# Attention and depthwise convolution in one kernel: longer groups, statistics ahead, and normalisation moved between engines

## The chip, the cores and the metric

One core of one Trainium2 chip runs the kernel. The metric is the device time of one execution in microseconds (us); the time of the kernel before is the median of 3 runs. The core has five engines that run their own instruction streams in order: TensorE (PE; its weight loads are shown apart as PEld), VectorE (DVE), ScalarE (ACT), GpSimd (POOL) and SyncE (SP). SP, ACT and POOL also issue DMAs; the queue of an engine is meant when "SP's queue" is said.

## The reference

Input x is (16, 384, 32, 32) in float32. Two layers follow each other, each on a group-normalised input (32 groups of 12 channels, per image) and with a residual:

```python
x = x + attention(gn(x), w_qkv, w_proj, b_proj)   # 8 heads of 48, 1024 tokens per image
x = x + dwconv7x7(gn(x), w_sym)                   # w_sym = mean of the weight's four rotations
```

The attention is softmax(q k^T / sqrt(48)) v, then a projection with a bias. The second group norm needs the whole image after the first layer.

## The kernel before, in words

Everything is float32. An image is three tiles of 128 channels x 1024 pixels (index k or o, NK = 3). Heads go in pairs: image b has four units u = 4b + p, and a unit has 16 steps n (two halves h of the queries, eight blocks i of keys). A step is one score product (s_step, L325: two matmuls into a PSUM tile of two banks, then ScalarE's exponential, L339) and one value product (av_step, L341, into an accumulator of its half). V carries a column of ones, so the sums of the exponentials come out as one row of the accumulator. `take` (L355) copies a finished half out of PSUM. The softmax's maximum isn't subtracted; a check at the end (L816) would start a second, general program (L613) if a sum were out of range, and in the runs here it isn't taken.

PSUM is three tiles ("s", L130) that scores, q/k, v and projection products rotate through, and two accumulators. The score product of step k therefore waits for the exponential of step k - 3.

After a unit, its sums go to DRAM and back as columns (sums_out, L361), VectorE inverts them (L372), they go out and come back spread over rows (L377), and VectorE divides (L383). After four units, proj_step (L393) makes three projection products from three tiles of o, into which the fourth unit's rows have been packed by DMA (L388); ScalarE adds the bias (L406), and a DMA on GpSimd's queue adds the residual x in place (L407). That is x1.

The group norms (class Stats, L188): bn_stats on VectorE per channel (L195), a trip through DRAM that gathers the 12 channels of a group into a row (L201, L203), an aggregate on VectorE (L208), 1/sigma by four one-column instructions on GpSimd (ve_x, L210 to L214, with a power of -0.5), and a trip back that spreads scale and shift over channels (L216, L220). For image 0's x and image 15's x1 there is a short way, groups_on_pe (L224): averages by small matmuls against mask blocks. `apply` (L259) normalises a tile: x by ScalarE, x1 into a tile xn by GpSimd (L261).

The convolution is 49 taps (conv_tap, L452): VectorE multiplies a shifted window of xn by one weight per channel and adds it into x1. 44 of the 48 tiles go this way; the tiles k = 1, 2 of images 14 and 15 (PE_TILES) are done by TensorE (conv_on_pe, L544), from shifted copies that are stored (conv_store, L526) and loaded again (L534), all of it after the last attention step. out is stored by GpSimd's queue (conv_end, L464).

The order on every engine is the order of the program text, written by a planner at build time. It keeps two clocks, `clock` for TensorE and `vclock` for VectorE, with fixed costs per piece of work. `after(wait, cost, f)` (L664) puts VectorE work into a heap with a due time; `catch_up(to)` (L691) emits due work and else taps, until vclock reaches `to`. The main loop (L858) goes over groups of GS = 4 steps: four score products, then four value products, then either a projection (`project`, L727) or, as a credit allows, up to two chunks of the next image's q/k (qk_step, L273) or v (v_step, L301), then catch_up. Image b + 1's x is loaded (begin_x, L761) when image b's last v chunk is out, since x has one buffer; it is loaded on SP's queue (L150), its statistics and norm follow through the heap. v has two buffers. The first image's q, k, v are all issued ahead of its steps. The last image ends in a different way (L922 on): sums by a matmul with ones (divide_at_once, L415), projection in four parts from unpacked o (proj_part, L425, with the weights w_proj_4), residual and bias on VectorE (L439), groups_on_pe.

Of the kernel before, what the change touches and what calls it, by code (L numbers as in the profile page):

```python
# [10 lines left out]
F32 = mybir.dt.float32  # L11
# [33 lines left out]
def kernel(  # L45
# [64 lines left out]
    def run(general):  # L110
        tag = "g" if general else "f"
        with ExitStack() as stack:
# [11 lines left out]
            epool = pool("epool", 6)  # L124
# [13 lines left out]
            PE_K = [NK - 1, NK - 2]  # L138
            PE_TILES = [(b, k) for b in (B - 2, B - 1) for k in PE_K]

# [6 lines left out]
            def load_x(b):  # L147
                xns[b] = xpool.tile([P, NK, N], F32, tag="x", name=f"x_{b}")
                for k in range(NK):
                    nc.sync.dma_start(  # L150
                        xns[b][:, k, :], x[b, k * P : (k + 1) * P].rearrange("p h w -> p (h w)")
                    )
# [12 lines left out]
            nc.sync.dma_start(wp, w_proj_t.rearrange("(k p) c -> p k c", p=P))  # L165
# [7 lines left out]
            vs = []  # L173
            for i in range(2):
                t = wpool.tile([P, NT, VW], F32, name=f"v_{i}")
                nc.gpsimd.memset(t, 1.0)
                vs.append(t)
# [4 lines left out]
            mhalf = wpool.tile([P, NK], F32, name="mhalf")  # L182
            nc.gpsimd.memset(mhalf, -0.5)

# [3 lines left out]
            class Stats:  # L188
# [16 lines left out]
                def groups(self):  # L205
# [3 lines left out]
                    ve = small.tile([GROUPS, 1], F32, tag="ve", name=f"ve_{self.name}")  # L209
                    nc.gpsimd.tensor_scalar(ve, mv[:, 1:2], EPS, None, ALU.add)  # L210
                    af = small.tile([GROUPS, 2], F32, tag="af", name=f"af_{self.name}")
                    nc.gpsimd.tensor_tensor(af[:, 0:1], ve, mhalf[0:GROUPS, 0:1], ALU.pow)
                    nc.gpsimd.tensor_tensor(af[:, 1:2], mv[:, 0:1], af[:, 0:1], ALU.mult)
                    nc.gpsimd.tensor_scalar(af[:, 1:2], af[:, 1:2], -1.0, None, ALU.mult)  # L214
# [9 lines left out]
                def groups_on_pe(self, masks):  # L224
# [29 lines left out]
                    nc.gpsimd.tensor_tensor(self.sc[:, :, 0], d, mhalf, ALU.pow)  # L254
# [4 lines left out]
                def apply(self, dst, src, k, engine=None):  # L259
# [11 lines left out]
                    )  # L271

# [28 lines left out]
            def v_step(b, t2):  # L301
# [11 lines left out]
                for j in range(2):  # L313
                    dst = vs[b % 2][:, 2 * t2 + j, 0 : HEADS * (D + 1)]
                    nc.scalar.copy(  # L315
                        dst.rearrange("p (h d) -> p h d", d=D + 1)[:, :, 0:D],
                        ps[:, j, 0:C].rearrange("p (h d) -> p h d", d=D),
                    )

            def v_of(u, i, j):  # L320
                b, p = divmod(u, NP)
                c = (2 * p + j) * (D + 1)
                return vs[b % 2][:, i, c : c + 64]
# [90 lines left out]

            def divide_at_once(u, h):  # L415
# [6 lines left out]

            late, pps = {}, {}
# [28 lines left out]
            def conv_tap(b, k, dy, dx):  # L452
                (oy, iy), (ox, ix) = region(dy, dx)
                acc = x1s[b, k].rearrange("p (h w) -> p h w", w=W)[:, oy, ox]
# [199 lines left out]
            clock, vclock = 0.0, 0.0  # L654
# [3 lines left out]
            GS = 4  # L658
            PER_B = 2 * NT * NP

            def now():
                return max(clock, vclock)
# [7 lines left out]
            def us_tap(dy, dx):  # L670
                late_us = 0.06 if active[0][0] >= B - 2 else 0.0
                return ((H - abs(dy)) * (W - abs(dx)) + (130 if len(active) > 1 else 270)) / 940 + late_us

            def tap():
# [3 lines left out]
                if not active:  # L678
                    return 0.0
                b, k, n = active[0]  # L680
                took = us_tap(*TAPS[n])
# [8 lines left out]

            def catch_up(to):  # L691
                nonlocal vclock
                while vclock < to:
# [8 lines left out]
                    else:  # L702
                        vclock = min([to] + [t[0] for t in later[:1]])

# [21 lines left out]

            def project(b):  # L727
# [6 lines left out]
            def x1_part(b, k):  # L734
# [4 lines left out]
                if k == NK - 1:  # L739
                    st.gather()  # L740
                    after(7.0, 0.8, lambda: x1_groups(b, st))

            def x1_groups(b, st):
                st.groups()
                after(9.0, 0.0, lambda: x1_chains(b, st))

            def x1_chains(b, st):
                on_pe = [t for t in PE_TILES if t[0] == b]
                for k in range(NK - 1, -1, -1):
                    tail = b == B - 1  # L750
                    conv_begin(st, b, k, (nc.gpsimd, None, nc.vector)[k] if tail else nc.gpsimd)
# [9 lines left out]
            def begin_x(b):  # L761
                load_x(b)
                after(10.0, 3.8, lambda: x_channels(b))

            def x_channels(b):
# [4 lines left out]
                after(12.0, 0.8, lambda: x_groups(b, st))  # L770

            def x_groups(b, st):
                st.groups()
                after(35.0, 0.0, lambda: x_apply(b, st))

            def x_apply(b, st):
                for k in range(NK):
                    st.apply(xns[b][:, k, :], xns[b][:, k, :], k)
                ready[b] = now() + 6.0

            def finish(u):
                sums_out(u)
                if u < U - 1:
                    after(7.0, 0.3, lambda: finish2(u))
# [5 lines left out]
            def finish3(u):  # L790
                b, p = divmod(u, NP)
                divide(u)
                if p == NP - 1:
                    proj.append((now() + 4.0, b))

            def queue(b):
                chunks.extend(("qk", b, i) for i in range(4))
                chunks.extend(("v", b, i) for i in range(2))
                chunks.extend(("qk", b, i) for i in range(4, 6))
                chunks.extend(("v", b, i) for i in range(2, 4))  # L800
# [5 lines left out]
            st.groups_on_pe(masks_0.rearrange("p (b c) -> p b c", c=P))  # L806
# [5 lines left out]
            while chunks:  # L812
                issue(chunks.popleft())
            vclock = clock
# [41 lines left out]

            credit = 0.0
            for n0 in range(0, NS, GS):  # L858
                b, r = divmod(n0, PER_B)
# [5 lines left out]
                for n in range(n0, n0 + GS):  # L865
                    s_step(n)
                if n0 == NS - 2 * GS:
                    after(3.5, 4.2, lambda: None)
                    divide_at_once(U - 1, 0)
                if n0 == NS - GS:  # L870
                    for o in range(NK):
                        proj_part(B - 1, o, (0, 1))
# [123 lines left out]
```

## Time and profile before

| what | value |
|---|---|
| median of 3 runs | 3024.0 us (3023.43 to 3024.72) |
| the profiled execution | 3021.88 us, its span 3020.0 us |
| PE, DVE, ACT, POOL busy | 98%, 87%, 43%, 24% of the span |
| scores L331, values L347 on PE | 948.6 us, 935.4 us |
| q/k L280, v L306, projection L398 on PE | 506.8, 254.5, 235.7 us |
| taps L455 on DVE | 2379.2 us, 2156 of them |
| exponentials L339 on ACT | 967.0 us, 1024 of them |
| xn L261 on POOL | 198.0 us, 46 of them, 4309 ns mean |
| ve_x L210 on POOL | 313.8 us, 30 of them, 10461 ns mean |
| mean clock granted to PE | 0.994 |

The span runs from the first to the last instruction that the profile shows. In a group's line stand the source line, the engine, the operation, output and input tiles by their names in the program, the count, then the busy time in us and the mean of one in ns; a time in brackets is how long the engine was idle before it, and what ended that. An engine's busy time counts overlapping instructions once. In the stretches, PEclk is the share of full speed that TensorE's clock was granted.

### The profile page before, as it was taken

What the parts mean: (1) busy time and instruction counts of PE and PEld (TensorE: products, weight loads), DVE (VectorE), ACT (ScalarE), POOL (GpSimd) and SP (SyncE); (2) the same over time, 40 slices, a digit from 0 to 9 for tenths busy, and PEclk for the clock granted to TensorE, in tenths of its full rate; (3) what the DMA queues carried; (4) which work ended last, traced back from release to release, by engine and by line L of the source; (5) the groups of instructions that cost most, each with busy time, mean ns of one, the idle gap of its engine ahead of it and who ended that gap; (6) DMA issues with size and microseconds to landing.
All of it is one profiled execution on the core that took longest, in us unless ns stands there. A gap on an engine that the chain in (4) does not pass through costs nothing.

```text
span 3020.0 us, 30559 instructions
## 1 busy us (share of the span) xinstructions
PE 2970.3 (98%) x11658; PEld 1166.2 (39%) x11658; DVE 2616.1 (87%) x2553; ACT 1298.7 (43%) x1469; POOL 728.3 (24%) x426
## 2 busy tenths in 40 slices
PE   7999999999999999999999999999999999999978
PEld 4333343433334343343434334343433434333333
DVE  1101898997999999999999999999999999999788
ACT  1534535354453545435353453535445353544400
POOL 1021004020140604215060320505133060411500
PEclk9999999999999999999999999999999999999989
DMA  2113031121312112131211313122131312212234
GB/s 70 38 23 67 15 66 37 39 53 33 67 36 58 23 52 51 36 70 39 52 30 36 66 36 66 42 46 37 36 66 36 66 37 51 37 43 38 89 83 114
DMA packets 68332, 149.42 MB, mean 49 GB/s; under 512 B 30880, under 2 KB 33168, under 8 KB 66640
## 3 DMA queue, kind: packets, MB, share of 16 engines
q1 hardware_dynamic: 47536, 90.80, 12.2%
q0 software_dynamic: 18560, 52.31, 7.8%
q10 hardware_dynamic: 2080, 4.26, 0.6%
q8 instruction: 94, 1.54, 0.2%
q14 instruction: 62, 0.51, 0.1%
HBM read 99.35 MB, written 29.49 MB: 43 GB/s over the span
## 4 chain that ended last, share of the span: by engine, by line
PE 90%; DVE 5%; issue 3%; POOL 1%; DMA 1%; ACT 0%; POOLq 0%; SPq 0%; DVEq 0%
PE ps_s L331 29%; PE acc L347 29%; PE ps_qk L280 16%; PE ps_v L306 8%; PE ps_proj L398 8%; DVE x L455 4%; POOL ve_x L210 1%; DMA wc<-in_w_conv 0%; PE ps_st_x L236 0%; DVE bs_x L195 0%; DMA out<-x 0%; DVE x L570 0%; DMA sums<-sum 0%; DMA sum<-o 0%; DVE o L383 0%
## 5 line engine op out<-in xcount | busy, mean ns | idle before, releaser
L455 DVE SCALAR_TENSOR_TENSOR x<-xn,wsym,x 128x960 f32<-128x960 f32 (+9 forms) x2156 | 2379.2, 1175 | 19.5 <-POOL xn L261 17.6
L339 ACT ACTIVATE e<-ps_s 128x1024 f32<-128x1024 f32 x1024 | 967.0, 1030 | 395.0 <-PE ps_s L331 390.1
L331 PE MATMUL ps_s<-qk 48*128 48x512 f32 x4096 | 948.6, 602 | 2.2 <-ACT e L339 2.2
L347 PE MATMUL acc<-e,v 128*64 128x512 f32 x4096 | 935.4, 598 | 0.0
L331 PEld LDWEIGHTS ps_s<-qk 48*128 48x128 f32 x4096 | 373.1, 186 | 566.8 <-issue 430.6
L347 PEld LDWEIGHTS acc<-e,v 128*64 128x64 f32 x4096 | 271.5, 136 | 632.4 <-issue 561.0
L280 PE MATMUL ps_qk<-x,wqk 128*128 128x512 f32 x1152 | 506.8, 596 | 2.3 <-DVE x L261 2.3
L407 POOL DMA_DIRECT2D x<-in_x x45 | 39.6, 881 | 1414.8 <-ACT x L406 1414.8
L280 PEld LDWEIGHTS ps_qk<-x,wqk 128*128 128x128 f32 x1152 | 217.0, 190 | 284.9 <-issue 278.3
L210 POOL TENSOR_SCALAR ve_x<-mv_x 32x1 f32<-32x1 f32 x30 | 313.8, 10461 | 44.4 <-DVE mv_x L208 43.3
L287 ACT COPY qk<-ps_qk 128x1024 f32<-128x1024 f32 x96 | 97.2, 1012 | 463.4 <-PE ps_qk L280 463.4
L306 PE MATMUL ps_v<-wv,x 128*128 128x384 f32 x768 | 254.5, 488 | 0.0
L398 PE MATMUL ps_proj<-o,wp 128*128 128x512 f32 x540 | 235.7, 595 | 0.2 <-DVE bs_x L195 0.2
L358 ACT COPY o<-acc 128x512 f32<-128x512 f32 x128 | 75.1, 587 | 307.2 <-PE acc L347 307.2
L261 POOL TENSOR_SCALAR xn<-x,sc_x 128x1024 f32<-128x1024 f32 x46 | 198.0, 4309 | 33.5 <-DMA sc_x<-gr_x 33.1
L195 DVE BATCH_NORM_STATS2 bs_x<-x 128x6 f32<-128x512 f32 x192 | 120.2, 680 | 98.8 <-DMA x<-in_x 98.7
L306 PEld LDWEIGHTS ps_v<-wv,x 128*128 128x128 f32 x768 | 144.7, 190 | 113.6 <-issue 20.3
L372 DVE RECIPROCAL rec<-sums 128x16 f32<-128x16 f32 x63 | 15.8, 250 | 185.4 <-DMA sums<-sum 185.3
L398 PEld LDWEIGHTS ps_proj<-o,wp 128*128 128x128 f32 x540 | 101.4, 190 | 134.4 <-issue 131.4
L315 ACT COPY v<-ps_v 128x384 f32<-128x384 f32 x128 | 55.1, 483 | 196.9 <-PE ps_v L306 196.9
L406 ACT ACTIVATE x<-ps_proj,bp 128x1024 f32<-128x1024 f32 x45 | 50.1, 1114 | 192.6 <-PE ps_proj L398 175.0
L383 DVE TENSOR_TENSOR o<-o,inv 128x1024 f32<-128x1024 f32 x63 | 76.6, 1216 | 55.5 <-DMA inv<-inv 34.0
(70 smaller groups left out, 486.1 us busy)
## 6 DMA issues: line engine op xcount, KB each, us to landing
inv<-inv SPq DMA_DIRECT2D x126, 256.0 KB
x<-in_x SPq DMA_DIRECT2D x48, 512.0 KB
x<-in_x POOLq DMA_DIRECT2D x48, 512.0 KB, 5.5
out<-x POOLq DMA_DIRECT2D x48, 512.0 KB, 3.5
qk<-qk SPq DMA_DIRECT2D x96, 128.0 KB
sh<-xd SPq DMA_DIRECT2D x38, 160.0 KB
o<-o SPq DMA_DIRECT2D x90, 64.0 KB
sh<-xd ACTq DMA_DIRECT2D x26, 160.0 KB
```

The source lines that it names most:

```text
L195: nc.vector.bn_stats(self.bs[:, k, 6 * h : 6 * h + 6], src[:, h * HALF : (h + 1) * HALF])
L210: nc.gpsimd.tensor_scalar(ve, mv[:, 1:2], EPS, None, ALU.add)
L261: engine.tensor_scalar(dst, src, self.sc[:, k, 0:1], self.sc[:, k, 1:2], ALU.mult, ALU.add)
L280: nc.tensor.matmul(ps[:, h, :], lhsT=wqk[:, k, s, t, :], rhs=xns[b][:, k, h * HALF : (h + 1) * HALF], start=(k == 0), stop=(k == NK - 1),)
L287: nc.scalar.copy(halves(qks[u][:, s, :]), ps)
L306: nc.tensor.matmul(ps[:, j, 0:C], lhsT=xns[b][:, k, t * P : (t + 1) * P], rhs=wv[:, k, :], start=(k == 0), stop=(k == NK - 1),)
L331: nc.tensor.matmul(ps[:, j, :], lhsT=qks[u][r, 1, i * P : (i + 1) * P], rhs=qks[u][r, 0, h * HALF : (h + 1) * HALF], start=True, stop=True,)
L339: nc.scalar.activation(es[n], ps, AF.Exp, scale=SCALE)
L347: nc.tensor.matmul(accs[u, h][64 * j : 64 * j + 64, :], lhsT=v_of(u, i, j), rhs=e[:, j, :], start=(i == 0), stop=(i == NT - 1),)
L383: nc.vector.tensor_tensor(os_[u], os_[u], invs.pop(u), ALU.mult)
L398: nc.tensor.matmul(ps[:, h, :], lhsT=wp[:, t, o * P : (o + 1) * P], rhs=os_[NP * b + t][:, h * HALF : (h + 1) * HALF], start=(t == 0), sto ...
L455: nc.vector.scalar_tensor_tensor(acc, xn1s[b, k].rearrange("p (h w) -> p h w", w=W)[:, iy, ix], wsym[:, k, dy + PAD, dx + PAD : dx + PAD + 1],
```

## The change

- **Groups.** An image's 64 steps go in groups of 7, the last of 8, with eight exponential buffers instead of six. A projection or chunks may now follow the score half of a group as well as the value half (`other`).
- **v** has one buffer. The four v chunks of image b are issued together behind the first score half of image b, and only then is x of image b + 1 loaded.
- **x of images 1 to 15** is loaded on GpSimd's queue.
- **Statistics of x for images 2 to 15** are made during image 0: their tiles are loaded once more on GpSimd's queue into x1's buffers, bn_stats is taken, and all scales are computed in one go and kept (x_sc). Image 1 keeps its own way.
- **ScalarE normalises** x1 as well as x (image 0 and 15's x1 on three engines), at a fixed place: behind a group's score half, one image's norm at a time (`applies`).
- **1/sigma** in Stats.groups: a bit-trick first value and three Newton steps on VectorE, in place of the four GpSimd instructions.
- **Image 0 ends like image 15** (FAST): four-part projection, residual on VectorE, groups_on_pe behind the first score half of image 1. Its weights are loaded at the start and replaced in image 1.
- **The last image's end** is reordered: the fourth unit's second half is divided between parts of the projection. The lone tile (15, 0) is summed into two accumulators in turn (tap_of_two).
- Costs and waits of the planner change with it.

```diff
-            epool = pool("epool", 6)
+            epool = pool("epool", 8)
...
+            FAST = (0, B - 1)
+            LONE = (B - 1, 0)
...
+                queue = nc.gpsimd if b else nc.sync
                 for k in range(NK):
-                    nc.sync.dma_start(
+                    queue.dma_start(
...
+            def inverse_sigma(dst, mean, var, name):
+                nc.vector.tensor_scalar(half, var, EPS, 0.5, ALU.add, ALU.mult)
+                nc.vector.tensor_scalar(
+                    y.bitcast(I32), half.bitcast(I32), 1, None, ALU.logical_shift_right
+                )
+                nc.vector.tensor_scalar(
+                    y.bitcast(I32), y.bitcast(I32), -1.0, float(MAGIC), ALU.mult, ALU.add
+                )
+                for _ in range(3):
+                    nc.vector.tensor_tensor(t, y, y, ALU.mult)
+                    nc.vector.tensor_tensor(t, t, half, ALU.mult)
+                    nc.vector.scalar_tensor_tensor(y, t, 1.5, y, ALU.subtract, ALU.mult)
+                nc.vector.tensor_tensor(dst[..., 1], mean, y, ALU.mult)
+                nc.vector.tensor_scalar(dst[..., 0], y, -1.0, None, ALU.mult)
...
+            def stream_in(b, k):
+                many[b, k] = rpool.tile([P, N], F32, tag="x1", name=f"xs_{b}_{k}")
+                nc.gpsimd.dma_start(
+                    many[b, k], x[b, k * P : (k + 1) * P].rearrange("p h w -> p (h w)")
+                )
+            def stream_stats(b, k):
+                t = many.pop((b, k))
+                for h in range(2):
+                    nc.vector.bn_stats(
+                        many["bs"][:, b - 2, k, 6 * h : 6 * h + 6], t[:, h * HALF : (h + 1) * HALF]
+                    )
...
+            SIZES = [7] * 8 + [8]
...
             def x1_groups(b, st):
                 st.groups()
-                after(9.0, 0.0, lambda: x1_chains(b, st))
+                applies.append((now() + 10.0, lambda: x1_chains(b, st)))
...
-                    conv_begin(st, b, k, (nc.gpsimd, None, nc.vector)[k] if tail else nc.gpsimd)
+                    conv_begin(st, b, k, (nc.gpsimd, None, nc.vector)[k] if b in (0, B - 1) else None)
...
             def begin_x(b):
                 load_x(b)
-                after(10.0, 3.8, lambda: x_channels(b))
+                if b == 1:
+                    after(10.0, 3.8, lambda: x_channels(b))
+                else:
+                    applies.append((now() + 14.0, lambda: x_apply(b, None)))
...
+            for n, bk in enumerate(every):
+                after(4.0 * n, 0.0, lambda bk=bk: stream_in(*bk))
+                after(4.0 * n + 10.0, 1.3, lambda bk=bk: stream_stats(*bk))
+            after(4.0 * len(every) + 14.0, 0.0, stream_gather)
+            after(4.0 * len(every) + 34.0, 3.6, stream_groups)
...
+            def fast_finish(b):
+                proj_part(b, 0, (NP - 2,))
+                divide_at_once(NP * b + NP - 1, 1)
+                for o in range(1, NK):
+                    proj_part(b, o, (NP - 2,))
+                x1_stats[b] = Stats(f"x1_{b}")
+                for o in range(NK):
+                    proj_part(b, o, (NP - 1,))
+                    residual(b, o)
+                    x1_stats[b].channels(x1s[b, o], o)
...
+                for n in range(n0, n0 + size):
                     s_step(n)
+                if r == 0 and b - 1 == FAST[0]:
+                    fast_end(b - 1)
+                if r == 0:
+                    for i in range(NT // 2):
+                        issue(("v", b, i))
+                ending = b in FAST and r + size == PER_B
+                if ending:
+                    catch_up(clock)
+                    divide_at_once(NP * b + NP - 1, 0)
                     for o in range(NK):
-                        proj_part(B - 1, o, (0, 1))
+                        proj_part(b, o, (0, 1))
+                else:
+                    if applies and applies[0][0] <= clock:
+                        applies.popleft()[1]()
+                    other(r + size)
+                for n in range(n0, n0 + size):
                     av_step(n)
...
+                if ending:
+                    catch_up(clock)
+                    fast_finish(b)
+                else:
+                    other(r + size)
```

## The prediction

> **What bounds the kernel now.** First the page, busy time (its first part) and the chain that ended last (its fourth).
>
> ```profile
> PE 2970.3 (98%) x11658; PEld 1166.2 (39%) x11658; DVE 2616.1 (87%) x2553; ACT 1298.7 (43%) x1469; POOL 728.3 (24%) x426
> PE 90%; DVE 5%; issue 3%; POOL 1%; DMA 1%; ACT 0%; POOLq 0%; SPq 0%; DVEq 0%
> ```
>
> TensorE is the bound. Second, stretches of one image in the steady part (columns: stretch, then busy us and count of PE, weight loads, DVE, ACT, POOL, then clock, DMA share, GB/s).
>
> ```profile
> 963.70:1141.80 178.10, 178.10 (x670) 69.50 (x668) 174.68 (x169) 81.33 (x92) 53.09 (x25) 1.00 0.20 47
> ```
>
> An image costs 178.1 us of TensorE, and VectorE has 174.7 us of work in it: two engines 3.4 us apart. A saving on TensorE counts only if VectorE's work falls too.
>
> Third, the timeline of TensorE and of its weight loads, to see what a group of four costs beyond its matmuls (start, duration, idle before).
>
> ```profile
> 161.69 3.70 PE L331 MATMUL ps_s<-qk 48*128 48x512 f32 x16
> 165.32 3.65 PE L347 MATMUL acc<-e,v 128*64 128x512 f32 x16
> 168.90 3.70 PE L331 MATMUL ps_s<-qk 48*128 48x512 f32 x16
> ```
>
> ```profile
> 164.00 0.19 PEld L331 LDWEIGHTS ps_s<-qk 48*128 48x128 f32 x2 [0.29 <-ACT e L339]
> 165.32 0.20 PEld L347 LDWEIGHTS acc<-e,v 128*64 128x64 f32 x4 [0.76 <-issue]
> 168.90 0.30 PEld L331 LDWEIGHTS ps_s<-qk 48*128 48x128 f32 x4 [0.81 <-issue]
> ```
>
> A group lasts 168.90 - 161.69 = 7.21 us. Inside a half, weight loads come 0.429 us apart, eight intervals a half, so 16 x 0.429 = 6.86 us is matmul. The rest, 0.35 us, is lost at the two turns between scores (L331) and values (L347), where the weight load shows the 0.76 and 0.81 us gaps.
>
> Fourth, the timeline at the end: TensorE, GpSimd and VectorE.
>
> ```profile
> 2869.79 3.65 PE L347 MATMUL acc<-e,v 128*64 128x512 f32 x16
> 2875.34 1.10 PE L418 MATMUL ps_sum<-o,masks 128*128 128x512 f32 x2 [1.90 <-DVE inv L420]
> 2878.31 8.09 PE L431 MATMUL ps_proj<-o,wp 128*128 128x512 f32 x12 [1.87 <-DVE o L383]
> ...
> 2898.20 7.53 PE L431 MATMUL ps_proj<-o,mat 128*128 128x512 f32 x10 [10.94 <-DVE o L421]
> 2905.66 5.98 PE L557 MATMUL ps_conv<-sh,mat 128*32 128x512 f32 x56
> ```
>
> ```profile
> 2788.99 38.41 POOL L210 TENSOR_SCALAR ve_x<-mv_x 32x1 f32<-32x1 f32 x1 [12.72 <-DVE mv_x L208]
> ```
>
> ```profile
> 2846.16 1.22 DVE L383 TENSOR_TENSOR o<-o,inv 128x1024 f32<-128x1024 f32 x1 [18.85 <-ACT e L339]
> ```
>
> From the last value product (2873.4) to the first convolution piece (2905.66) TensorE takes 32.2 us for 17.5 us of matmuls. The cause lies 85 us earlier: a one-column GpSimd addition (ve_x) takes 38.4 us while VectorE runs taps; so xn of image 14 is late; SP waits to store it (a 29.9 us wait at L527) with the inverse sums queued behind it; VectorE stands idle 18.85 us; its taps slip, and the reciprocal that TensorE needs at 2878 comes at 2894. After that 100 us of convolution on TensorE set the end; VectorE stops with it.
>
> **Turns.** 16 groups an image become 9: 16 x 7 = 112 fewer turns x 0.35 = **-39.2 us**, all on the path. Does ScalarE follow a run of seven? In the same timeline exponentials start 1.24 us after the first score (1000.97, 1002.21) and 4 take 3.77 us: the first 1.03, later ones 0.913 each, against 0.858 for a score step. With three PSUM buffers, score k waits for exponential k-3. At k = 4 the weight load already waits 0.06 us (0.29 against 0.23), and no matmul is delayed. At k = 7 the wait is 0.06 + 3 x 0.055 = 0.23 us; a weight load comes 0.43 us ahead of its matmul and lasts 0.19, so 0.24 us hide it. The eight-group loses 0.05 us. Cost 0; if the cover is thinner, up to 0.17 us a group, 24 us in all.
>
> **Single v buffer, order of chunks.** The same v matmuls (15.5 us an image) run in one block behind the first seven scores; their copies (0.86 us a pair) finish ahead of the value products that read them. 0.
>
> **Normalisation on ScalarE, Newton.** xn leaves GpSimd (44 of 46 applications, 4.3 us mean) for ScalarE: three take 3.5 us (1.17 each). ScalarE is done with seven exponentials 7.75 us after the group began and has nothing due before 13.5 us, so 3.5 us fit. What is queued behind a waiting normalisation is the next group's exponentials, and TensorE waits for those. x's scale goes away per image; x1's needs its four GpSimd instructions replaced by some 13 small VectorE ones at about 0.2 us apart (0.16 each in the row of L248 to L252): 2.6 us. VectorE per image: 174.7 - 3.65 (x statistics) - 0.79 (one aggregate) + 2.6 = 172.9 us, against TensorE's new 178.1 - 2.45 = 175.7. It still fits, by 2.8 us. The wait itself: x1's scale is on chip some 7.3 us after the last Newton step (90.23 to about 97.5 for the two small DMAs); the plan grants 10 us and then up to a group more. Steady cost 0; if VectorE lags its plan, up to 3 us an image.
>
> **x by GpSimd's queue.** Three issues of about 0.53 us; they wait for TensorE's last v block, with stores and small gathers behind them. The Trainium skill ("SBUF — State Buffer", Who interferes with whom) speaks against this: a DMA issued by GpSimd has its descriptors made there and can starve while VectorE holds the shared port. The trace: the 45 residual loads of the same queue (L407) cost 0.88 us of GpSimd each, with taps running, and land after 5.5 us. If they starved as ve_x does (10.5 us mean, 38.4 at worst), the load, normally on chip in 8 us and needed some 24 us after it starts, would be 0 to 22 us late for its image. I take the row: 0. SP loses those loads, which waited there for v too (332 us in all, L150) with sums behind them; no TensorE gap hangs on that today, so no gain. SP gains three weight loads, needed an image later: 0.
>
> **First image: statistics.** 42 tiles come in behind image 1's load on GpSimd's queue, which itself waits for v (about 76 us). In VectorE's order 14 tiles' statistics stand ahead of image 1's own, and four more ahead of its aggregate. A tile's pace: image 1's load today moved 1.7 MB in 5.4 us.
>
> ```profile
> GB/s 0 0 0 205 68 150 273 273 328 423 437 437 369 396 314 287 246 232 369 464 437 137 164 164 191 164 191 164 137 191 191 164 82 27 109 27 55 54 8 0
> ```
>
> That (window 72 to 84 us, 40 slices) is 317 GB/s, 1.65 us a tile. Image 1's statistics then end near 112, gather 118, aggregate and Newton 124, scale on chip 131, while ScalarE reaches that normalisation at 127; exponentials follow 1 to 2 us late: **+1 us**. At 400 GB/s it is 0, at the 227 GB/s of the first 20 us +10. The statistics themselves (42 x 1.28 us) lie in VectorE's idle time. The scales of images 2 to 15 go out and back in 8-byte pieces (1,536 and 5,376 of them, where today 384 land in 4.2 and 2.8 us) behind image 2's load: an estimate of 18 to 30 us by these rows, against 25 us until needed: **+2 us** (0 to 8).
>
> **First image: fast end.** Image 0 ends like image 15: two sum products (2 x 1.06), projection in four parts instead of three (15.65 / 9 = 1.74 each, three more: 5.2), statistics on TensorE (1.72 + 0.65 + 2.71 = 5.1): **+12.4 us** on the path. It brings the first tap from 299 to about 260 us, which TensorE, the bound, can't use. VectorE must be on time there (its reciprocal and multiply, 4.05 us, lie beside 4.4 us of matmuls); otherwise up to 6 more.
>
> **The end.** With Newton the 38 us addition is gone, and so is the chain behind it. The new order puts 1.74 + 1.06 + 3.5 + 5.2 = 11.5 us of matmuls and about 0.3 of waiting in place of 32.2: -20.3; I leave 2 for VectorE being late: **-18 us**. What is late next is nothing before the convolution, 100 us of TensorE as before. The second accumulator of the lone tile shortens VectorE only, which in that stretch has about 63 us of work: 0.
>
> None of these waits can be a gain: they shorten nothing on TensorE.
>
> **Sum**, on the span of 3020.0: -39.2 + 1 + 2 + 12.4 - 18 = -41.8, so 2978.2. The profiled execution took 3021.88, 1.88 over its span; the median of the runs is 2.1 above that. So 2982.
>
> **Rivals.** (A) The sum, 2972 to 2991: 0.56. (B) The first image costs more: slow tiles (+10), late scales (+8), a late reciprocal: 2991 to 3002. For it: nothing in the trace streams so; against: VectorE is idle there. 0.20. (C) ScalarE waits in order for an x1 scale, 1 to 2 us an image in 14 images, 2996 to 3010; for it: 2.8 us of VectorE slack is little; against: today VectorE reaches its reciprocals early (in 900 to 2700 us it waits 31 us there for the sums). 0.12. (D) The same place turned into the bound, slower than before: if VectorE's work passes TensorE's image by so much that each normalisation holds the exponentials 4 us or more, 14 x 4 = 56 us: 3038. It decides from 42 / 14 = 3 us an image, that is, a VectorE image over 178.7 us where I count 172.9; taps (162.4 us for 147, 1.105 each) would have to be 4% slower, and without GpSimd's normalisation they should be faster. 0.07. (E) The edit does more than I count, 2965 to 2972, with no lateness at the end and a full clock there (0.68 today in those 32 us): 0.05.
>
> **Numbers.** 2982; 2968 to 3005 leaves out part of C, all of D and part of E. About 0.2% (6 us) is what a measurement of this kernel tells from no change: faster 0.89, same 0.04, slower 0.07.
>
> **What would show it.** Right: S-to-S of seven steps 12.36 us; an image 175.7 us of TensorE with no gap; ve_x gone; under 14 us from the last value product to the first convolution piece; VectorE near 173 us an image. Wrong: TensorE gaps released by exponentials behind a normalisation (B in image 0 or 1, C and D in all), scores slower than 0.86 us at the sixth or seventh step, VectorE at 100%.

## The result and the profile after

The changed kernel takes 2979.78 us (median of 4 runs, 2977.55 to 2982.38); the kernel before took 3024.29 us on the same measure. The ratio is 0.9853 (95% interval 0.9836 to 0.9871), 44.5 us less. The forecast was 2982. The profiled execution took 2982.38 us, its span is 2980.2, so the span fell by 39.8 us. The two differences are not the same because single executions scatter: the profiled one of the kernel before lay 2.4 us under its median, that of the changed kernel 2.6 over.

The page of the changed kernel, busy time:

```profile
PE 2943.7 (99%) x11702; PEld 1191.2 (40%) x11702; DVE 2626.3 (88%) x2771; ACT 1326.4 (45%) x1509; POOL 200.7 (7%) x304
```

TensorE is the bound as before, busy for 99% of the span. GpSimd fell from 728 to 201 us, and ScalarE rose by only 28. That is no account of the gain yet: neither of the two is the bound. The gain is read stage by stage.

A stretch in the steady part (columns as in the prediction), then TensorE's timeline in image 0, two score halves and the value half between them:

```profile
1303.00:1479.00 176.00, 176.00 (x669) 70.28 (x668) 171.03 (x177) 83.57 (x95) 8.51 (x13) 1.00 0.20 47
```

```profile
83.37 6.28 PE L425 MATMUL ps_s<-qk 48*128 48x512 f32 x28
89.58 6.23 PE L441 MATMUL acc<-e,v 128*64 128x512 f32 x28
95.74 4.56 PE L425 MATMUL ps_s<-qk 48*128 48x512 f32 x20
```

A group of seven lasts 95.74 - 83.37 = 12.37 us. The same chunk recurs 175.85 us later in nearly every image from image 2 on, where it was 178.1, and VectorE works 171.0 us in such a stretch.

The end, on TensorE:

```profile
2846.47 7.09 PE L441 MATMUL acc<-e,v 128*64 128x512 f32 x32
2853.49 1.98 PE L524 MATMUL ps_proj<-o,wp 128*128 128x512 f32 x4
2855.31 1.02 PE L513 MATMUL ps_sum<-o,masks 128*128 128x512 f32 x2
2856.16 3.60 PE L524 MATMUL ps_proj<-o,wp 128*128 128x512 f32 x8
2859.60 5.52 PE L524 MATMUL ps_proj<-o,mat 128*128 128x512 f32 x12
2865.05 5.98 PE L651 MATMUL ps_conv<-sh,mat 128*32 128x512 f32 x56
```

From the end of the last value product (2846.47 + 7.09 = 2853.56) to the first convolution piece (2865.05) it is 11.5 us, and no line shows a wait in brackets. Before, it was 32.2, with the same number of products (24 for the projection, 2 for the sums): the rest was waiting and a lower clock (0.68 granted there).

The one place where TensorE stood still in the middle is image 1. The same moment on TensorE, ScalarE and GpSimd:

```profile
302.26 12.26 PE L374 MATMUL ps_qk<-x,wqk 128*128 128x512 f32 x24 [3.75 <-ACT x L296]
```

```profile
300.97 3.51 ACT L296 ACTIVATE x<-x,x_sc 128x1024 f32<-128x1024 f32 x3 [7.13 <-DMA x_sc<-gr_all]
```

```profile
268.11 1.68 POOL L153 DMA_DIRECT2D x<-in_x  x3 [15.64 <-ACT v L409]
...
272.75 3.83 POOL L357 DMA_DIRECT2D gr_all<-af_all  x4 [1.91 <-DVE x L549]
297.16 3.27 POOL L363 DMA_DIRECT2D x_sc<-gr_all  x3 [20.58 <-issue]
```

Read from the bottom: GpSimd was held at image 2's load until the last v chunk was copied; the scales of images 2 to 15 went out behind it; they took some 20 us to land in DRAM (the 20.58 us ahead of the last row, which names no releaser here; the same row of experiment 12 names this DMA); ScalarE waited 7.13 us at the place fixed for image 2's normalisation, and TensorE 3.75 us for ScalarE.

The whole span, from the same points of both traces:

| stretch | before | after | difference | forecast |
|---|---|---|---|---|
| start to the first q/k product | 23.69 | 22.64 | -1.05 | 0 |
| to the last value product's end | 2849.75 | 2830.9 | -18.8 | -23.8 |
| to the first convolution piece | 32.2 | 11.5 | -20.7 | -18 |
| to the end | 114.3 | 115.15 | +0.8 | 0 |

What the first row's microsecond comes from stays open. The second row is taken apart below, by experiments 4 and 11.

### The profile page after: what moved, and what is told of

Its sections match the earlier page's. It is cut to its first block, busy times and chain, and to the rows that moved or that the text cites. A ratio compares the mean times of both kernels' runs of the same rounds, so it can differ in the third digit from the quotient of the medians.

```text
span 2980.2 us, 30719 instructions
## 1 busy us (share of the span) xinstructions
PE 2943.7 (99%) x11702; PEld 1191.2 (40%) x11702; DVE 2626.3 (88%) x2771; ACT 1326.4 (45%) x1509; POOL 200.7 (7%) x304
## 4 chain that ended last, share of the span: by engine, by line
PE 76%; issue 11%; DMA 1%; DVE 1%; POOL 0%; ACT 0%; SPq 0%; POOLq 0%; DVEq 0%
PE ps_s L425 24%; PE acc L441 24%; PE ps_qk L374 14%; PE ps_v L400 7%; PE ps_proj L492 6%; PE ps_conv L651 1%; DVE x L549 1%; DMA x<-in_x 0%; DMA out<-x 0%; DMA sh<-xd 0%; DVE bs_x L230 0%; DMA x_sc<-gr_all 0%; DMA gr_x<-af_x 0%; DVE sum L549 0%; POOL out L559 0%
## 5 line engine op out<-in xcount | busy, mean ns | idle before, releaser
L549 DVE SCALAR_TENSOR_TENSOR x<-xn,wsym,x 128x960 f32<-128x960 f32 (+9 forms) x2132 | 2328.0, 1166 | 49.0 <-ACT xn L296 47.5
L433 ACT ACTIVATE e<-ps_s 128x1024 f32<-128x1024 f32 x1024 | 954.4, 1048 | 357.1 <-PE ps_s L425 353.4
L425 PE MATMUL ps_s<-qk 48*128 48x512 f32 x4096 | 918.4, 597 | 0.0
L441 PE MATMUL acc<-e,v 128*64 128x512 f32 x4096 | 910.7, 596 | 0.0
L441 PEld LDWEIGHTS acc<-e,v 128*64 128x64 f32 x4096 | 281.1, 137 | 608.5 <-issue 600.5
L492 PE MATMUL ps_proj<-o,wp 128*128 128x512 f32 x504 | 220.0, 595 | 0.0
L400 PEld LDWEIGHTS ps_v<-wv,x 128*128 128x128 f32 x768 | 146.0, 192 | 110.3 <-ACT e L433 11.4
L153 POOL DMA_DIRECT2D x<-in_x x45 | 24.0, 539 | 1536.7 <-ACT v L409 1535.2
L319 DVE BATCH_NORM_STATS2 bs_all<-xs 128x6 f32<-128x512 f32 x84 | 52.5, 680 | 83.8 <-DMA xs<-in_x 83.7
L230 DVE BATCH_NORM_STATS2 bs_x<-x 128x6 f32<-128x512 f32 x108 | 69.0, 684 | 50.5 <-DMA x<-in_x 40.9
L651 PE MATMUL ps_conv<-sh,mat 128*32 128x480 f32 (+3 forms) x896 | 96.1, 587 | 2.5 <-DMA sh<-xd 2.5
L501 POOL DMA_DIRECT2D x<-in_x x42 | 36.5, 870 | 468.7 <-ACT x L500 463.6
```

The source lines that it names most:

```text
L230: nc.vector.bn_stats(self.bs[:, k, 6 * h : 6 * h + 6], src[:, h * HALF : (h + 1) * HALF])
L400: nc.tensor.matmul(ps[:, j, 0:C], lhsT=xns[b][:, k, t * P : (t + 1) * P], rhs=wv[:, k, :], start=(k == 0), stop=(k == NK - 1),)
L425: nc.tensor.matmul(ps[:, j, :], lhsT=qks[u][r, 1, i * P : (i + 1) * P], rhs=qks[u][r, 0, h * HALF : (h + 1) * HALF], start=True, stop=True,)
L433: nc.scalar.activation(es[n], ps, AF.Exp, scale=SCALE)
L441: nc.tensor.matmul(accs[u, h][64 * j : 64 * j + 64, :], lhsT=v_of(u, i, j), rhs=e[:, j, :], start=(i == 0), stop=(i == NT - 1),)
L492: nc.tensor.matmul(ps[:, h, :], lhsT=wp[:, t, o * P : (o + 1) * P], rhs=os_[NP * b + t][:, h * HALF : (h + 1) * HALF], start=(t == 0), sto ...
```

## The experiments

Under test are the terms of the prediction's sum: the turns, image 0's fast end, the late scales of image 2, and the end, with the Newton steps as its cause. The rivals: that the gain rests on another part (statistics made ahead, x's new queue, ScalarE's normalisation); that a group of seven is beyond or short of ScalarE's limit; and that ScalarE's waits in order could make the kernel slower than before (rival D). Ratios are against the kernel before, with 95% intervals. "Images" are TensorE's time from one image's v chunks to the next image's.

**1. Groups of four** in the changed kernel.

```diff
-            SIZES = [7] * 8 + [8]
+            SIZES = [4] * 16
```

(The credit of a group is scaled with it, and the places of the late loads go to 36, 44 and 52.)

> The changed kernel with 16 groups of four steps instead of nine of seven or eight; all else as changed. Theory (the turns): 112 turns more at 0.35 us each, 39 us, so 2980 + 39 = 3019 us, and an image of 178.3 us of TensorE instead of 175.85; VectorE's image stays near 171 us. Rival (the gain came from relieving VectorE and GpSimd, and TensorE was only following them): 2980 to 2985 us, an image near 176 us.

3037.93 us, ratio 1.0044 (1.003 to 1.0057). An image takes 178.35 us instead of 175.85: 2.50 us for 7 more turns of scores to values and back, 0.357 each. That is the price in the prediction, so the turns are right. The kernel lost 58, not 39, because the late scales of image 2 now hold TensorE for 17.2 us instead of 3.75, and those of image 1 for 3.3 where they held it for none. ScalarE:

```profile
305.81 3.50 ACT L296 ACTIVATE x<-x,x_sc 128x1024 f32<-128x1024 f32 x3 [17.75 <-DMA x_sc<-gr_all]
```

The scales are as late after image 2's load as before the edit (33 us: 305.81 against the load's issue at 272.89; in the changed kernel 300.97 against 268.11). What moved is ScalarE's place: it is the first score half behind a set time, and so jumps by up to a group when the group length changes. ScalarE reaches it 15.2 us after the load here, 25.7 us after it in the changed kernel.

**2. Groups of eight.**

```diff
-            SIZES = [7] * 8 + [8]
+            SIZES = [8] * 8
```

> The changed kernel with eight groups of eight steps. Theory (a turn costs 0.35 us, and the weight loads' lead still hides ScalarE's slower pace at the eighth score): one turn fewer an image, 16 x 0.35 = 5.6 us, so 2974 us; the score half lasts 7.06 us. Rival (seven is the longest run that ScalarE can follow): each of the 128 score halves loses 0.05 us or more, 6 us in all, so 2980 us or slower, and score halves over 7.1 us.

2990.26 us, 0.9886 (0.9871 to 0.9901): slower than seven, where faster was expected. Yet an image takes 175.50 us, one turn less as worked out. The loss is again mainly in waits of the first images: 13.4 us of TensorE for image 2's scales, for which ScalarE stands 17.5 us, and 2.6 us for image 1's. ScalarE's place lies 15.4 us after the load here too, so longer groups brought it forward just as shorter ones did. Another 2.7 us are lost in the convolution at the end (117.8 us against 115.15). The edit also leaves two places, 40 and 48, for the late loads of shifted copies where there were three, and TensorE waits for such a copy (3.1 us); that the missing place is the cause is not shown.

So eight isn't past ScalarE's limit. The reason is seen in the changed kernel's own group of eight, in the weight loads of its score half (idle time before in brackets):

```profile
1278.86 0.19 PEld L425 LDWEIGHTS ps_s<-qk 48*128 48x128 f32 x2 [0.30 <-ACT e L433]
...
1279.77 0.51 PEld L425 LDWEIGHTS ps_s<-qk 48*128 48x128 f32 x4 [0.35 <-ACT e L433]
...
1282.52 0.33 PEld L425 LDWEIGHTS ps_s<-qk 48*128 48x128 f32 x4 [0.53 <-ACT e L433]
1283.61 0.20 PEld L441 LDWEIGHTS acc<-e,v 128*64 128x64 f32 x4 [0.76 <-issue]
```

The rows are those of the fourth, fifth and eighth score and of the first value product. From the fourth on, the loads start 0.91 to 0.92 us apart, at ScalarE's pace, while a score step lasts 0.858. Their lead over the matmuls shrinks by 0.06 us a step and is not used up at the eighth: the half, from its first load at 1276.54 to 1283.61, lasts 7.07 us, as long as eight steps and a turn without any wait (8 x 0.858 + half of 0.357 = 7.04).

**3. Image 0 ends like the others**, only image 15 fast.

```diff
-            FAST = (0, B - 1)
+            FAST = (B - 1,)
```

(The weights are loaded packed at once, and image 0's x1 is normalised by ScalarE.)

> The changed kernel in which image 0 ends as the images between do (projection in three parts through the plan, x1 statistics by way of DRAM, norm on ScalarE); only image 15 ends fast. Theory (the fast end of image 0 is paid on TensorE and bought nothing there): 2.1 + 5.2 + 5.1 us of TensorE work and 2.7 us of a lower clock behind it go, so 2980 - 15 = 2965 us. Rival (it is needed, since VectorE starts its taps earlier by it and is close to full): 2980 us or slower, with the loss late in the kernel.

2969.68 us, 0.9819 (0.9806 to 0.9833): 10 us faster than the change, where 15 were expected. It is a balance of three things: the fast end is gone, the wait for image 2's scales is gone with it (2.57 us on ScalarE, no gap on TensorE), and a new wait has come, 6.85 us on TensorE, since image 0's x1 scales now come by DMA, with the convolution's small preparation loads ahead of them on GpSimd's queue. Experiments 4 and 11 take the three apart. ScalarE:

```profile
311.34 3.51 ACT L291 ACTIVATE xn<-x,sc_x 128x1024 f32<-128x1024 f32 x3 [9.36 <-DMA sc_x<-gr_x]
```

**4. Image 2's normalisation 12 us later.**

```diff
-                    applies.append((now() + 14.0, lambda: x_apply(b, None)))
+                    applies.append((now() + (26.0 if b == 2 else 14.0), lambda: x_apply(b, None)))
```

> The changed kernel with image 2's normalisation one group later, so that ScalarE doesn't wait for the scales that come through DRAM. Theory: the one wait of ScalarE that TensorE feels in the changed kernel (7.1 us on ScalarE, 3.75 us idle and a lower clock for 12 us on TensorE) goes: 2980 - 5.4 = 2974.5 us. Rival (the wait only moves, to the q/k chunks of image 2 that come later): 2980 us.

2973.09 us, 0.9831 (0.9817 to 0.9844): 6.7 us faster than the change. No gap is left there. With 3.75 us idle and 1.7 more in the products behind it at a lower clock (12.26 against 10.57 us for the same 24 products), the wait cost 5.4; the sign and the size are confirmed. One more microsecond of the difference is image 1's v block, which ran in 17.42 us here and in 18.41 in the changed kernel.

**5. Newton in the kernel before, for image 14's x1 alone.** The four GpSimd instructions are replaced there, and nothing else.

```diff
+                    if self.name == f"x1_{B - 2}":
+                        inverse_sigma(af.unsqueeze(1), mv[:, 0:1], mv[:, 1:2], self.name)
+                    else:
...
```

> The kernel before, with one thing changed: image 14's x1 scale (one of 30) takes 1/sigma from the Newton steps on VectorE instead of the four GpSimd instructions. Theory (the 32.2 us between the last value product and the convolution come from that one GpSimd addition of 38.4 us): the wait falls to some 15 us and the kernel takes 3024 - 17 = 3007 us, with VectorE's 18.85 us of idle time gone. Rival (the end is slow because VectorE's taps are behind anyway, or because of the old order of the last products): 3022 to 3024 us.

3019.69 us, 0.9986 (0.9979 to 0.9992): 4.3 us instead of 17. The 38 us addition is gone, but the wait at the end stays. GpSimd and TensorE in this run:

```profile
2802.75 34.54 POOL L291 TENSOR_SCALAR xn<-x,sc_x 128x1024 f32<-128x1024 f32 x3 [1.69 <-DMA sc_x<-gr_x]
```

```profile
2873.69 3.65 PE L377 MATMUL acc<-e,v 128*64 128x512 f32 x16
...
2896.05 7.21 PE L461 MATMUL ps_proj<-o,mat 128*128 128x512 f32 x10 [10.89 <-DVE o L451]
```

Three tiles of xn, next on GpSimd, took 34.5 us. Nearly all of it is the first: it lasts 32.2 us and ends 1.1 us after VectorE's run of taps does (2833.9), and the other two take 1.19 each. In the kernel before, the same three tiles took 3.55 us, since VectorE was idle by then. So the store of xn came at 2835, late once more, with the inverse sums behind it on SP's queue. From the last value product to the convolution it is 25.9 us here: the prediction's cause gives 6.4 of the 20.7 us by itself.

**6. The change with 1/sigma on GpSimd**, the opposite edit: GpSimd's four instructions in place of the Newton steps.

> The changed kernel with the four GpSimd instructions back in place of the Newton steps. Theory (the additions starve under taps, about 19 us per x1 scale, and now ScalarE waits in order for the scale with the exponentials behind it; today the scale lies ready 9.6 us ahead): 3 to 5 us lost in most images, 3020 to 3050 us, with TensorE gaps released by ScalarE in the steady images. Rival (ScalarE's fixed place has room enough, or VectorE's saved 2 us weigh as much): 2978 to 2985 us.

3066.40 us, 1.0139 (1.0123 to 1.0154): 87 us slower than the change, and slower than before. GpSimd, VectorE and ScalarE in the middle of the run:

```profile
1016.91 17.98 POOL L246 TENSOR_SCALAR ve_x<-mv_x 32x1 f32<-32x1 f32 x1 [4.66 <-DVE mv_x L243]
```

```profile
1033.60 1.21 DVE L481 TENSOR_TENSOR o<-o,inv 128x1024 f32<-128x1024 f32 x1
1047.21 3.68 DVE L553 SCALAR_TENSOR_TENSOR x<-xn,wsym,x 128x1024 f32<-128x1024 f32 x3 [12.41 <-ACT xn L300]
```

```profile
1043.67 3.50 ACT L300 ACTIVATE xn<-x,sc_x 128x1024 f32<-128x1024 f32 x3 [7.07 <-DMA sc_x<-gr_x]
```

The addition ends at 1034.89, 0.1 us after VectorE has run out of work (1034.81), and VectorE has run out because its next taps need the very xn that hangs on this addition. It takes 16 us on average, ScalarE waits in order, and TensorE idles 3.2 to 4.6 us an image, 6.8 in the last; images take 181 to 184 us. This is rival D's mechanism, reached through a late scale instead of VectorE's load, and it costs more (87 us, where D counted 56). So with ScalarE's places where this plan has them, the Newton steps are needed; whether later places would do as well wasn't run.

**7. Statistics image by image** up to image 10, instead of one stream in image 0 (the stream is still made).

```diff
-                if b == 1:
+                if b <= 10:
                     after(10.0, 3.8, lambda: x_channels(b))
```

> The changed kernel in which images 1 to 10 take x's statistics for themselves as image 1 does (six bn_stats, aggregate, Newton on VectorE, two trips through DRAM); the statistics in image 0 are still made. VectorE's image grows by 6.4 us to 177.4, over TensorE's 175.85. Theory (VectorE's room is what lets TensorE's saving stand): the 9 images from 2 to 10 lose 1.5 us or more each once the slack of the first ones is used, 2985 to 3000 us, with VectorE at 99%. Rival (VectorE's slack is not needed): 2978 to 2982 us.

3000.51 us, 0.9922 (0.9909 to 0.9936): 20.7 us slower than the change. The sum was met, at its upper edge; its mechanism was not. Two steady images (stretch columns as above):

```profile
1840.00:2192.00 352.00, 352.00 (x1338) 141.22 (x1337) 351.11 (x362) 167.37 (x190) 17.10 (x26) 1.00 0.21 47
```

TensorE doesn't wait in the middle: VectorE is full at 175.6 us an image and falls behind, and its taps are needed only at the end. Some 8 us of the loss lie there (TensorE's last product ends at 2977.3, VectorE's last instruction at 2990.3), and 12 us in images 1 and 2, where TensorE has gaps of 11.4 and 3.5 us (the changed kernel 3.75 there). The larger one is not VectorE's load but a late scale again: image 2's own statistics are gathered behind the convolution's preparation on GpSimd's queue (at 318.2 us). So the statistics made ahead count, as the prediction's budget said, but a deficit of VectorE is paid once at the end.

**8. x on SP's queue again**, all else changed.

```diff
-                queue = nc.gpsimd if b else nc.sync
+                queue = nc.sync
```

> The changed kernel with x of every image loaded on SP's queue, as before. Theory: no steady difference, since the loads are on chip long before ScalarE normalises; but GpSimd's queue no longer waits for v ahead of image 0's tiles and of the scales, so the waits in images 0 and 1 shrink by up to 5 us: 2975 to 2980 us. Rival (SP's queue then holds the sums and inverses back behind x's wait for v): 2985 us or more, with VectorE waiting for inverses.

3042.39 us, 1.0059 (1.0046 to 1.0073): 62.6 us slower than the change, where none or a small gain was expected; the rival had named the cause. SP's queue and TensorE in one image:

```profile
1131.88 3.77 SPq L390 DMA_DIRECT2D qk<-qk  x6
1151.21 1.31 SPq L153 DMA_DIRECT2D x<-in_x  x3
1152.62 0.37 SPq L468 DMA_DIRECT2D inv<-rec  x1
...
1164.12 3.70 SPq L482 DMA_DIRECT2D o<-o  x6
```

```profile
1167.15 17.39 PE L492 MATMUL ps_proj<-o,wp 128*128 128x512 f32 x36 [3.61 <-DMA o<-o]
```

SP is done with q and k at 1135.65 and stands at x's load until 1151.21, when TensorE's v block ends (1151.18). The inverse sums of the last unit stand behind the load, so o is packed late and the projection waits, 3.6 us in this image; images take about 181 us.

**9. Experiment 5 and image 14's x1 normalised by ScalarE**, in the kernel before.

> The kernel before, with image 14's x1 scale by Newton steps as in the run before it, and image 14's three x1 tiles normalised by ScalarE instead of GpSimd. Corrected theory (with Newton alone GpSimd's three normalisations took 34.5 us in the place of the addition's 38.4, so SP stayed blocked and VectorE idle; both have to leave GpSimd): VectorE's 10 us of idle time at 2834 us and TensorE's wait of 10.9 us behind the last value product go, 3019.7 - 11 to 14 = 3006 to 3009 us. Rival (VectorE's taps ahead of the last reciprocal are there by the plan, whatever GpSimd does): 3017 to 3020 us with the 10.9 us still there.

3011.58 us, 0.9956 (0.9942 to 0.997), where 3006 to 3009 were expected. TensorE at the end:

```profile
2877.81 3.65 PE L377 MATMUL acc<-e,v 128*64 128x512 f32 x16
...
2893.51 5.98 PE L587 MATMUL ps_conv<-sh,mat 128*32 128x512 f32 x56
```

Now 12.0 us lie between the last value product and the convolution: the whole 20 us of the end, in the old kernel and in its old order. The kernel gains 12.8, for some is lost elsewhere, by the profiles: 4 us in image 15, where the normalisation stands ahead of an exponential (a gap of 2.2 us at 2813, and a lower clock behind it), 3 behind an equal gap at 506 us, which the kernel before has as well but at full clock, and 2 behind the convolution's start. The cause of the old end is both GpSimd instructions: whichever comes first meets the taps and is held. The normalisation moved alone, with the addition left, wasn't run.

**10. The change with x1 of images 1 to 14 normalised by GpSimd.**

```diff
-                    conv_begin(st, b, k, (nc.gpsimd, None, nc.vector)[k] if b in (0, B - 1) else None)
+                    conv_begin(st, b, k, (nc.gpsimd, None, nc.vector)[k] if b in (0, B - 1) else nc.gpsimd)
```

> The changed kernel with x1 of images 1 to 14 normalised by GpSimd again (Newton stays on VectorE). Theory (GpSimd's reads starve under taps: 18 us for three tiles in the middle, some 30 at the end; TensorE is not waiting for xn in the middle, but at the end SP's store of xn and the inverses behind it are late, and VectorE's taps slow down a little): image 175.85 us still, an end that is 10 to 20 us later, 2990 to 3000 us. Rival (where xn is made doesn't matter once Newton is on VectorE): 2978 to 2982 us.

2978.45 us, 0.9846 (0.9832 to 0.9859): no difference from the change. xn of image 14 took 19.98 us on GpSimd, but the new order starts it at 2772.6, early enough for its store to go out at 2790, and the end lasts 11.5 us as before the edit. Moving the normalisation to ScalarE is not what the gain rests on, once Newton and the new order are there.

**11. No waits in the first images**: experiment 3, and the convolution's preparation moved from image 1 to image 3.

```diff
-                if b == 1 and r == 0:
+                if b == 3 and r == 0:
                     conv_prepare()
```

> The changed kernel with image 0 ending slowly, as in the third run, and the convolution's small loads on GpSimd's queue moved from image 1 to image 3. Theory (in the third run ScalarE waited 9.4 us for image 0's x1 scale because those 25 small DMAs stood ahead of its gather on GpSimd's queue, and TensorE lost 6.85 us and 1.7 us of clock by it): 2969.7 - 8.5 = 2961 us, no TensorE gap between 22 us and the last value product. Rival (the scale is late for VectorE's sake): 2969 us.

2958.99 us, 0.9784 (0.977 to 0.9797): 20.8 us faster than the change and the fastest of all. After the first q/k product TensorE has no gap until the last value product. The scales of image 2 come in time here (a wait of 1.25 us on ScalarE). Against experiment 4, which has no wait in image 1 either, the fast end of image 0 costs 14.1 us. From the first q/k product to the last value product this run takes 2810.7 us, and with neither a fast end nor a wait in it that stretch shows what the turns are worth: 39.0 us less than before.

**12. Groups of eight on top of 11**, with the x of images 1 and 2 normalised later (20 instead of 12, 26 instead of 14 us).

> The run before it with eight groups of eight steps, and the norms of images 1 and 2 allowed to start later (8 and 12 us), since longer groups reach their fixed place sooner after a load. Theory (a turn is 0.35 us, and the second run lost only by waits in images 0 and 1): one turn fewer in each of 16 images, 2961 - 5.6 = 2955 us, 175.5 us an image. Rival (eight is past what ScalarE can follow, and waits come up elsewhere): 2961 us or more.

2984.68 us, 0.9868 (0.9853 to 0.9883), not under 11's time: images take 175.50 us again, but image 1 takes 196.75, with a gap of 12.5 us for image 2's normalisation. GpSimd in this run, and in run 11:

```profile
238.74 1.57 POOL L153 DMA_DIRECT2D x<-in_x  x3 [74.22 <-ACT v L404]
240.30 3.28 POOL L323 DMA_DIRECT2D ch_all<-bs_all  x3
...
282.63 3.27 POOL L358 DMA_DIRECT2D x_sc<-gr_all  x3 [18.18 <-DMA gr_all<-af_all]
```

```profile
185.54 3.46 POOL L323 DMA_DIRECT2D ch_all<-bs_all  x3 [14.94 <-DVE bs_all L314]
...
237.11 1.62 POOL L153 DMA_DIRECT2D x<-in_x  x3 [38.70 <-ACT v L404]
```

With eights the load of image 2 falls ahead of the gather of the statistics in GpSimd's queue; GpSimd stands 74 us at the load, and the whole trip of the scales begins behind it. In run 11 the gather goes ahead of it, 55 us earlier. The convolution at the end is longer too, 118.0 us against 112.3, with waits for shifted copies of 3.8 and 0.5 us (0.4 in run 11) and two places for their loads, as in experiment 2. Each of the two losses alone eats the 5.6 us that eight should bring by the periods; what it brings without them wasn't run.

## Why the prediction was right

**Bound and turns: right.** 16 groups became 9, an image 175.85 us (forecast 175.7), a group of seven 12.37 (12.36). Experiment 1 gives 0.357 us a turn pair by another route. The lead of the weight loads hides ScalarE's pace, at seven and at eight steps. From the first q/k product to the last value product the traces add up like this:

| step | stretch | difference | forecast |
|---|---|---|---|
| before | 2849.75 | | |
| experiment 11: turns, no fast end, no wait | 2810.7 | -39.0 | -39.2 |
| experiment 4: with image 0's fast end | 2824.55 | +13.85 | +12.4 |
| the change: with the wait for scales | 2830.9 | +6.35 | +3 (2 and 1) |

All the terms that were put at 0 on TensorE lie in the first step; together they come to about nothing.

**VectorE's budget: right, 2 us too high.** 171.0 us against 172.9. It fits TensorE's image, and with the x statistics left in (experiment 7) it no longer does. What was not said: exceeding the image by little shows at the end only.

**Image 1's own scale: right.** ScalarE was to reach the normalisation at 127 and find the scale at 131; it came free at 128.3, waited 2.17 us and began at 130.45. TensorE shows no gap there: 0 instead of +1.

**Scales of image 2: mechanism right, term mis-sized.** Of the 0 to 8 us the forecast took +2; it is 5.4 by the trace and 6.7 by experiment 4. From the load's issue to the scales on chip it takes 32.9 us (268.11 to 300.97), where 18 to 30 were set; they were needed after 25.7 (forecast 25). The forecast's count of the pieces was off as well: 1,536 is one of the four DMAs out, which together write the 42 KB that come back as 5,376 pieces.

**Fast end of image 0: right, one term missing.** +12.4 was forecast; 13.85 by the traces and 14.1 by the medians of experiments 4 and 11. The forecast counted its matmuls at full clock and nothing behind them: the v block that follows takes 17.42 us in experiment 4, where such a block takes 15.75. Its early taps bring TensorE nothing.

**The end: size right, reason half right.** -20.7 against -18 (VectorE was not late, so the 2 us kept for it were not needed). The step "with Newton the 38 us addition is gone, and so is the chain behind it" failed in experiment 5: with the addition gone, GpSimd's normalisation met the taps in its place, took 34.5 us instead of 3.55, and kept the chain. Experiment 9 removes both and has the gain. In the changed kernel the earlier place does for the normalisation what ScalarE does (experiment 10), so the size came out right for the change as a whole, and not because Newton alone removes the chain.

**x by GpSimd's queue: priced at 0, the row rightly taken.** The loads didn't starve beside the taps: 0.54 us each. But "no gain" compared it with SP's queue in the old order only. With v in one late block SP's place costs 62.6 us (experiment 8), so the queue is part of what the new order needs.

**Rivals.** B is seen in part: the first images cost 20.2 us where 15.4 were counted, 4.8 more, short of the 9 at which B begins. C and D didn't come: no x1 normalisation made TensorE wait. D's place is real, though: with the power on GpSimd it makes the kernel 1.4% slower than before (experiment 6).

**The sum was in part lucky.** On the span it is -39.8 against -41.8. Misses of +5.0 in the first images, -2.7 at the end and -1.05 ahead of the first q/k product have different causes and happen to offset each other in part.

## What to carry to other kernels

Count the turns between two kinds of matmul and price one from the gap of the weight loads; it is a saving on the bound that can be trusted if the second engine's work falls too. Where engines and queues run in order, a gain is lost at the first place where something that isn't ready stands ahead of something that is: after each edit, of a group length too, read the order on every queue that the moved step passes and where the fixed places fall, and give a fixed place more time than its slowest DMA trip. When a slow instruction on the late chain is removed, ask what stands next on the same engine and is slow for the same reason.

## What the runs showed of the hardware beyond that

- GpSimd beside VectorE's taps: a 32 x 1 addition took 18 us in the median of experiment 6 (0.18 to 0.57 us for the three of the same size behind it). The 13 of its 15 additions that met taps ended 0.1 us after VectorE's unbroken run of instructions did, after 18 to 23 us of it; the two that met no taps took 0.25 us. In experiment 5 one tile of normalisation was held for 32.2 us in the same way. It isn't always so long: in the kernel before, second and third tiles got through between taps, in 2.95 us each (857 to 874 us). The Trainium skill ("SBUF — State Buffer", Who interferes with whom) has a VectorE instruction with two SBUF inputs, which a tap is, contend with a GpSimd instruction that reads SBUF, over the port pair that the two engines share; the runs add that one short GpSimd instruction can be kept out over a run of some 16 such instructions.
- Small pieces: the four DMAs that write the scales to DRAM, 12, 12, 12 and 6 KB in 8-byte pieces, needed 18 to 21 us to land in the changed kernel, where a 512 KB load of x lands in 5.4; the way back, three DMAs of 14 KB, was on chip 3.8 us after its issue began (300.97 - 297.16). Why the way out is so slow is open.
- The clock: behind the 28 one-column statistics matmuls of image 0 with a gap of 0.64 us, it was granted at 0.60 for the next 7 us. A gap of 2.2 us that ends near 505 us left it at 1.00 in the profile of the kernel before; behind the same gap in that of experiment 5 it was 0.55 from 505 to 508 us and 0.67 from there to 514.
